# Three pairs of V projections, one block's stores and the last products of a cross-attention layer, rearranged

## The chip, the cores and the metric

The kernel runs on one core of a Trainium2 chip. The metric is device microseconds of one execution of the whole layer. A core has a matrix engine (TensorE, PE in the profile, with its weight loads shown as PEld), a vector engine (VectorE, DVE), a scalar engine (ScalarE, ACT), GpSimd (POOL) and SyncE (SP), which here issues most transfers. Each engine takes its instructions in the order in which the program lists them and waits by semaphores. Products are accumulated in PSUM, which has eight banks of 128 x 512 float32; data lie in SBUF.

## The reference

Four batches, 512 query rows, 512 context rows, width 512, 16 heads of 32, an inner width of 2048, all in float32:

```
x  = layer_norm(hidden) ;  q = x @ q_w + q_b ;  k = enc @ k_w + k_b ;  v = enc @ v_w + v_b
p  = softmax(where(mask, q k^T / sqrt(32), min))       # per head
h  = (p @ v) @ cproj_w + cproj_b + hidden
y  = gelu(layer_norm(h) @ fc_w + fc_b)                 # tanh form
out = h + y @ proj_w + proj_b
```

## The kernel before

Attention is cut into 16 units: a unit `w` is one batch (`w // 4`) and a group of four heads (128 columns). For each unit TensorE makes K (`prep_k`), Q (`prep_q`) and V (`prep_v`), each 128 columns wide. K and Q come out with the head columns on partitions, by four matmuls of 128 x 512. V comes out with the context rows on partitions, by 16 matmuls of 128 x 128 (L285): the context is the stationary side, the 128 columns of `v_w` the moving side. `prep_v_pair` makes V of two units at once, with 16 matmuls of 128 x 256 (L310) into two PSUM banks; each bank is then copied by ACT in two copies, one per unit (L314), and POOL adds the bias to each unit's V (`v_bias`, L321). Before the change units 10 and 11, 12 and 13, 14 and 15 are made so, and units 0 to 9 one by one.

Each unit has two blocks of 256 queries, so there are 32 blocks, `p = 2 * w + half`. In a block, TensorE makes the scores of four heads for two tiles of 128 queries (eight banks, L329); DVE adds the mask and takes each row's minimum of the negated scores (L335); ACT takes the exponential and the row sums (L339); DVE transposes 32 x 32 blocks into a tile `tb` (L347), takes the reciprocal of the sums, ACT spreads it over 32 columns (`rr`, L368), and DVE transposes this too into `tb` (L372). The 32-row blocks then change partitions into `pT` (or into `gt` or `xe`, which serve as further such buffers): POOL copies four of the pieces (L405) and SP issues 12 transfers for the others (L410). Two or three blocks later `attend` multiplies V by them on TensorE (`av`, L429) and DVE divides by the sums into `oT` (L434), which frees the buffer for the next exchange.

While DVE and ACT work on the softmax, TensorE is given other products. A table written by hand, `put(p, items...)`, lists the items of each block with a cost: 3.4 for a projection, 0 for things like a load or a normalisation. `block` calls `fill` at three places: after the last minima of the block (place 0), after the last transposition of `rr` (place 1), and after the exchange has been started (place 2, everything left). At places 0 and 1, `run` takes items while the cost already spent plus half the next one's is at most 3.4, so one projection and the cost-free items right behind it are taken. `next_` gives an item a cost of 0.01, so that it waits for the next place. What ACT and DVE have to do for an item stands in their own order at that place: the bias or copy that empties the bank on ACT, or in block 4 the affine part of batch 1's first normalisation (`ln1_affine`, four activations, L225), which that batch's Q products read.

PSUM banks go round in the order of use. A block uses one bank for `av`, eight for scores, and then one for each product; the first product behind the scores takes the bank of the block's first scores and waits until DVE has taken the minimum from it.

The first MLP layer, and the second for part of the batches, are done by Winograd's form of Strassen's product: seven block products instead of eight, with sums of blocks made ahead. `fc_sums` makes the sums of a pair of `fc_w` tiles on POOL (L622 and L625), ahead of the block that uses them, and for batch 0 stores them to DRAM from POOL's own queue (L714, L715), for the later batches to load. `proj_sums` (`pre`) makes those of a second-layer quarter on POOL; block 14 ends with `pre(0, 0)`.

The last two batches' second layer nests the form twice (`forty_nine`, matmuls of L904). The call named "4" is the last work of the program: seven products, the last two (`s4 w22` and `x22 t4`) into one bank, DVE's additions onto the residual in quarters of 128 x 128, and two stores of 128 x 256 by SP (L1028).

The steps that the change touches are `fc_sums` with the new `late`, `forty_nine`, its last caller in `project`, the `put` lines of blocks 0 to 8, 14 and 29, and the loop that calls `fc_sums`.

Of the kernel before, what the change touches and what calls it, by code (L numbers as in the profile page):

```python
# [53 lines left out]
def xattn_block(ctx: ExitStack, tc: tile.TileContext, x, rawT, encT, mask, q_w, k_w, v_w, c_w, fc_w, p_w, vecs, rows, out):  # L54
# [569 lines left out]
    def add(engine, o, x0, x1):  # L624
        engine.tensor_tensor(o, x0, x1, ALU.add)  # L625
# [77 lines left out]

    def fc_sums(ahead=2):

        while count[3] < len(fc_pairs) and count[3] < count[4] + ahead:
            b, c = fc_pairs[count[3]]
            if ("fcw", b, 2 * c + 1) not in S:
                return
            x, y = raw_pair(b, c)  # L710
            s = wsum[:, count[3] % 2]
            a_sums(x[:, :2], x[:, 2:], y[:, :2], y[:, 2:], s[:, 0], s[:, 1], y[:, :2], s[:, 2], nc.gpsimd)
            if b == 0:
                nc.gpsimd.dma_start(out=sums_dram[c, :, :3], in_=s)  # L714
                nc.gpsimd.dma_start(out=sums_dram[c, :, 3], in_=y[:, :2])  # L715
            S["ws", b, c] = s[:, 0], s[:, 1], y[:, :2], s[:, 2]
            count[3] += 1

    def fc_by_pair(b, c):
# [129 lines left out]
    def last_mlps():  # L849
# [38 lines left out]

        def forty_nine(b, name, o, x, w, free, i, parts=None):

# [24 lines left out]
            if parts:  # L915
                for n, h in enumerate(parts):
                    add(nc.vector, h, o[:, n], h)
            product(r34[:, 0], s4, w22)
            product(r34[:, 1], x22, t4)
            if parts:  # L920
                for n in (1, 2):
                    add(nc.vector, parts[n], r34[:, n - 1], parts[n])
                return
            add(nc.vector, o[:, 1:3], r34[:, :2], o[:, 1:3])
# [13 lines left out]
        def project(b, pairs, sums, turns, middle):  # L938
# [12 lines left out]
            def hid(i, j, t):  # L951
                return S["hid", b, 2 * i + t][:, j * HL : (j + 1) * HL]
# [70 lines left out]
            if b > SPLIT:  # L1023
                parts = [hid(1, 0, t)[:, ts(j, P)] for t in range(2) for j in range(2)]
                middle()
                forty_nine(b, "4", u2p, g22, t4, s3, 5, parts)
                for t in range(2):
                    nc.sync.dma_start(out=out[b, ts(2 + t, P), :HL], in_=hid(1, 0, t))  # L1028
                return
# [73 lines left out]
    def do(fn):  # L1103
        return [(0.0, fn)]

    def next_(fn):
        return [(0.01, fn)]
# [122 lines left out]
    k6, q6, v6 = A(6)  # L1230
    put(0, [(CHAIN, lambda: prep_v(1)), v2], do(lambda: (load_raw(1), store_rn(1))), [k2])
    put(1, [k3, (0.0, lambda: prep_q(1)), (CHAIN, lambda: (prep_v(3), load_enc(1)))], next_(lambda: load_rn(1)))
    put(2, [q2], [q3], do(lambda: ln1_rows(1, 0, 1)))
    put(3, [k4], do(lambda: ln1_rows(1, 2, 3)), [v4])
    put(4, [k5, v5], do(lambda: ln1_affine(1)))
    put(5, [q4, q5])
# [3 lines left out]
    c, t2 = C(0), turns2(0)  # L1240
    put(7, [v6, k], cb(0))
    put(8, x1, [q, v], x4)
    put(9, c[:1], do(lambda: attend(3, 1)), x2[:2], c[1:2], x2[2:], stat(0, 0), c[2:3], stat(0, 1),
# [9 lines left out]
    put(13, [k], some(2))  # L1253
    put(14, [q], some(2), x1, pre(0, 0))
    put(15, some(1), x2[:1], V(10, True), x2[1:2], do(lambda: load_raw(3)), some(2), do(lambda: (store_rn(3), load_rn(3))))
# [21 lines left out]
    put(28, some(3))  # L1277
    put(29, some(1), do(lambda: (fc_sums(), S["late"].pop()())), some(2), do(lambda: (store_out(0), load_mlp())))
    between[14, 1] = lambda: load_mlp(2)
# [5 lines left out]
    for p in range(2 * NW):  # L1285
# [6 lines left out]
        if p > 10:  # L1292
            fc_sums(1 if p == 29 else 2)
        while held_back:
# [73 lines left out]
```

## Time and profile before

| | us |
|---|---|
| median of 3 runs | 757.13 (755.95 to 757.17) |
| profiled execution | 758.21 |
| its span | 756.4 |
| TensorE busy in the span | 748.7 |
| VectorE busy | 617.6 |
| GpSimd busy | 403.6 |
| ScalarE busy | 341.0 |
| V of one unit, behind another projection | 3.57 |
| V of a pair, behind another product | 6.91 |

A row of the profile in order of time has the start and the duration in us, the engine, the line, the operation with output and inputs, shapes, how often it came in a row, and in square brackets the idle time of the engine before it and what ended that. A row of the chain has start, duration and what. A releaser is inferred from semaphore events; where an instruction waits for several, the one that came last is named, and it can be another. SPq and POOLq rows are the issue of a transfer, not its data.

### The profile page before, as it was taken

To read this page: it belongs to the slowest core of one execution; us is meant where nothing else is said; L and a number is where in the kernel's file an instruction comes from. 1 tells how busy PE (TensorE), PEld (TensorE's weight loads), DVE (VectorE), ACT (ScalarE), POOL (GpSimd) and SP (SyncE) were. 2 spreads that over 40 slices of the span, in tenths; PEclk is the share of its full clock that TensorE was granted. 3 is DMA by queue.
4 is the path that set the end of the run, shared out by engine and by line. 5 is a ranking of instruction groups with operands and counts; after the bars stand their busy time and mean duration, and the time that the engine had idled before them with its cause. 6 is when DMAs were issued, how large, how long until landed. Compare 5 with 4: busy or idle time off the path is not lost.

```text
span 756.4 us, 13322 instructions
## 1 busy us (share of the span) xinstructions
PE 748.7 (99%) x4514; PEld 536.2 (71%) x4514; DVE 617.6 (82%) x1229; ACT 341.0 (45%) x776; POOL 403.6 (53%) x401
## 2 busy tenths in 40 slices
PE   9999999999999999999999999999999999999997
PEld 6655555567567546675655776468888899988997
DVE  3889999879988779877987999949877987956865
ACT  2566766555874475648853578401302211022200
POOL 1536837468687987667868974532150014403153
PEclk9999999999999999999999999999999999999999
DMA  8988989467796797676756757766634402046001
GB/s 326 348 238 223 248 208 257 107 191 185 210 255 208 199 268 182 169 193 156 196 129 198 195 145 242 187 213 234 242 104 152 155 13 91 29 162 201 1 15 43
DMA packets 60836, 134.62 MB, mean 178 GB/s; under 512 B 11312, under 2 KB 17072, under 8 KB 60640
## 3 DMA queue, kind: packets, MB, share of 16 engines
q1 hardware_dynamic: 59024, 127.78, 58.7%
q0 software_dynamic: 1600, 5.97, 2.6%
q8 instruction: 36, 0.59, 0.3%
q14 instruction: 32, 0.26, 0.1%
q10 hardware_dynamic: 144, 0.02, 0.0%
HBM read 69.23 MB, written 11.02 MB: 106 GB/s over the span
## 4 chain that ended last, share of the span: by engine, by line
PE 95%; POOL 3%; DMA 1%; issue 0%; SPq 0%; DVE 0%; DVEq 0%; POOLq 0%
PE q L671 24%; PE r L904 10%; PE sc L329 8%; PE av L429 7%; PE acck L262 7%; PE accq L274 7%; PE accc L471 6%; PE accv L285 5%; PE accp L758 4%; PE accv L310 3%; PE q1p L965 2%; PE tp L169 1%; POOL pT L405 1%; PE q3j L777 1%; PE q1j L777 1%; PE q7j L777 1%
## 5 line engine op out<-in xcount | busy, mean ns | idle before, releaser
L339 ACT ACTIVATE ptt<-ptt,mn 128x512 f32<-128x512 f32 x256 | 181.7, 711 | 142.3 <-DVE mn L335 142.3
L335 DVE CUSTOM_DVE_ANT_0 ptt<-sc,mb 128x512 f32<-128x512 f32 x256 | 160.6, 682 | 19.9 <-PE sc L329 19.9
L347 DVE STREAM_TRANSPOSE tb<-ptt 128x1024 f32<-128x1024 f32 x128 | 153.3, 1217 | 0.0
L405 POOL COPY pT<-tb 32x1088 f32<-32x1088 f32 x96 | 104.7, 1091 | 35.1 <-DVE oT L434 11.6
L671 PE MATMUL q<-yT,gt 128*128 128x256 f32 x320 | 78.9, 379 | 0.0
L692 ACT ACTIVATE ga<-ga,vec 128x512 f32<-128x512 f32 x40 | 26.7, 714 | 93.3 <-DVE ga L625 93.3
L671 PEld LDWEIGHTS q<-yT,gt 128*128 128x128 f32 x320 | 60.7, 190 | 8.2
L329 PE MATMUL sc<-pbt 32*128 32x512 f32 x512 | 66.1, 614 | 0.0
L671 PE MATMUL q<-ys,gt 128*128 128x256 f32 x240 | 61.6, 379 | 0.0
L262 PE MATMUL acck<-xe,ptt 128*128 128x512 f32 x128 | 59.1, 605 | 0.0
L274 PE MATMUL accq<-xe,ptt 128*128 128x512 f32 (+1 forms) x136 | 58.1, 573 | 0.0
L671 PEld LDWEIGHTS q<-ys,gt 128*128 128x128 f32 x240 | 45.6, 190 | 6.2
L625 DVE TENSOR_TENSOR ga<-q,ga 128x512 f32<-128x512 f32 (+1 forms) x60 | 36.2, 603 | 15.8 <-PE q L671 12.9
L429 PE MATMUL av<-pT,v 128*32 128x256 f32 x768 | 46.4, 382 | 2.1 <-POOL gt L622 1.9
L339 ACT ACTIVATION_READ_ACCUMULATOR ptt<-ptt,mn 128x1 f32 x256 | 47.8, 187 | 0.0
L274 PEld LDWEIGHTS accq<-xe,ptt 128*128 128x128 f32 x136 | 25.0, 190 | 30.4 <-issue 23.0
L440 POOL TENSOR_TENSOR hid<-hid,row 128x512 f32<-128x512 f32 x18 | 23.5, 1332 | 42.2 <-DMA hid<-xa 42.2
L262 PEld LDWEIGHTS acck<-xe,ptt 128*128 128x128 f32 x128 | 23.4, 192 | 31.6 <-issue 23.0
L329 PEld LDWEIGHTS sc<-pbt 32*128 32x128 f32 x512 | 27.2, 183 | 25.5 <-issue 17.2
L471 PE MATMUL accc<-wc,oT 128*128 128x512 f32 x96 | 42.5, 597 | 0.0
L285 PEld LDWEIGHTS accv<-ptt,xe 128*128 128x128 f32 x320 | 37.0, 192 | 4.9 <-DVE mn L335 2.7
L321 POOL TENSOR_TENSOR v<-v,row 128x512 f32<-128x512 f32 x16 | 20.3, 1280 | 37.1 <-ACT v L290 29.7
(263 smaller groups left out, 1437.2 us busy)
## 6 DMA issues: line engine op xcount, KB each, us to landing
pT<-tb SPq DMA_DIRECT2D x288, 136.0 KB
pbt<-p_w_dram SPq DMA_DIRECT2D x40, 256.0 KB
gt<-ws SPq DMA_DIRECT2D x20, 512.0 KB
gt<-tb SPq DMA_DIRECT2D x48, 136.0 KB
xe<-tb SPq DMA_DIRECT2D x48, 136.0 KB
pbt<-fc_w_dram SPq DMA_DIRECT2D x24, 256.0 KB
gt<-fc_w_dram SPq DMA_DIRECT2D x20, 256.0 KB
ptt<-k_w_dram SPq DMA_DIRECT2D x16, 256.0 KB
```

Source lines behind the costliest of these rows:

```text
L262: nc.tensor.matmul(acc, S["wk", w][:, d, :], eT[:, d, :], start=(d == 0), stop=(d == ND - 1))
L274: nc.tensor.matmul(acc, S["wq", w][:, d, :], xT[:, d, c], start=(d == 0), stop=(d == ND - 1))
L285: nc.tensor.matmul(acc[:, ts(t, P)], eT[:, d, ts(t, P)], S["wv", w][:, d, :], start=(d == 0), stop=(d == ND - 1),)
L329: nc.tensor.matmul(S["sc", w, qt][h], qT[r, ts(qt, P)], kT[r, :], start=True, stop=True)
L335: nc.vector.tensor_tensor_reduce(out=s, in0=S["sc", w, qt][h], in1=S["mb", w // NG], scale=1.0, scalar=FMAX, op0=ALU.add, op1=ALU.min, acc ...
L339: nc.scalar.activation(s, s, AF.Exp, bias=mn, scale=-1.0, accum_out=S["sums", w][:, qt, h : h + 1])
L347: nc.vector.transpose(tv[:, qt % 2, 2 * k : 2 * k + 2], S["ps", w, qt, k])
L405: nc.gpsimd.tensor_copy(pT[ts(i, HD), i], tb[ts(i, HD), i])
L429: nc.tensor.matmul(av[ts(h, HD), : 2 * P].rearrange(shape, **kw), v[:, t, ts(h, HD)], p[t][h], start=(t == 0), stop=(t == NT - 1),)
L471: nc.tensor.matmul(acc, S["oT", b][:, g, ts(t, P)], wc[:, g, :], start=(g == 0), stop=(g == NG - 1))
L671: nc.tensor.matmul(o, x[:, k], y[:, k], start=(k == 0), stop=(k == 1))
L904: nc.tensor.matmul(r, x[:, c], w[:, c], start=(c == 0), stop=(c == NP // 2 - 1))
```

## The change

Three things change.

V of units 2 and 3, 4 and 5, 6 and 7 is made by `prep_v_pair`, in blocks 1, 4 and 8, and the K products of units 2, 3, 5, 7 and the Q product of unit 7 move so that blocks 0 to 8 keep two or three projections' worth of work each. In block 4 the list is now the pair and then the affine part of batch 1's normalisation, without a K product ahead of them; since the pair counts as one item of cost 3.4 and the affine part costs nothing, both are taken at place 0.

The stores of the sums of `fc_w` are put into a list and issued at once, except in block 14, where they are issued after `pre(0, 0)`.

In the last `forty_nine` the two last products get banks of their own, DVE's additions onto the residual are made in halves of two quarters, the store of each part is issued as soon as it is ready, the first two from ACT's queue, the last one, of 128 x 128, from SP's.

```
-    def fc_sums(ahead=2):
+    def fc_sums(ahead=2, hold=False):
...
             if b == 0:
-                nc.gpsimd.dma_start(out=sums_dram[c, :, :3], in_=s)
-                nc.gpsimd.dma_start(out=sums_dram[c, :, 3], in_=y[:, :2])
+                S["late"].append(lambda c=c, s=s, y=y: (
+                    nc.gpsimd.dma_start(out=sums_dram[c, :, :3], in_=s),
+                    nc.gpsimd.dma_start(out=sums_dram[c, :, 3], in_=y[:, :2]),
+                ))
+                if not hold:
+                    late()
...
+    def late():
+        while S["late"]:
+            S["late"].pop(0)()
...
             if parts:
-                for n, h in enumerate(parts):
-                    add(nc.vector, h, o[:, n], h)
+                r4 = half_tile(f"r4{name}_{b}").rearrange("p i (j n) -> p (i j) n", j=2)
+                first, second = parts
+                add(nc.vector, first, o[:, :2], first)
+                product(r34[:, 0], s4, w22)
+                add(nc.vector, first[:, 1], r34[:, 0], first[:, 1])
+                ready(nc.scalar, 0, slice(0, HL))
+                add(nc.vector, second, o[:, 2:], second)
+                ready(nc.scalar, 1, slice(P, HL))
+                product(r4[:, 0], x22, t4)
+                add(nc.vector, second[:, 0], r4[:, 0], second[:, 0])
+                ready(nc.sync, 1, slice(0, P))
+                return
             product(r34[:, 0], s4, w22)
             product(r34[:, 1], x22, t4)
-            if parts:
-                for n in (1, 2):
-                    add(nc.vector, parts[n], r34[:, n - 1], parts[n])
-                return
...
-    put(0, [(CHAIN, lambda: prep_v(1)), v2], do(lambda: (load_raw(1), store_rn(1))), [k2])
-    put(1, [k3, (0.0, lambda: prep_q(1)), (CHAIN, lambda: (prep_v(3), load_enc(1)))], next_(lambda: load_rn(1)))
+    put(0, [(CHAIN, lambda: prep_v(1)), k2], do(lambda: (load_raw(1), store_rn(1))), [k3])
+    put(1, [(CHAIN, lambda: prep_q(1))], V(2), do(lambda: load_enc(1)), next_(lambda: load_rn(1)))
     put(2, [q2], [q3], do(lambda: ln1_rows(1, 0, 1)))
-    put(3, [k4], do(lambda: ln1_rows(1, 2, 3)), [v4])
-    put(4, [k5, v5], do(lambda: ln1_affine(1)))
+    put(3, [k4], do(lambda: ln1_rows(1, 2, 3)), [k5])
+    put(4, V(4), do(lambda: ln1_affine(1)))
...
-    put(7, [v6, k], cb(0))
-    put(8, x1, [q, v], x4)
+    put(7, [k, q], cb(0))
+    put(8, x1, V(6), x4)
...
-    put(14, [q], some(2), x1, pre(0, 0))
+    put(14, [q], some(2), x1, pre(0, 0), do(late))
...
-    put(29, some(1), do(lambda: (fc_sums(), S["late"].pop()())), some(2), do(lambda: (store_out(0), load_mlp())))
+    put(29, some(1), do(lambda: (fc_sums(), late())), some(2), do(lambda: (store_out(0), load_mlp())))
...
-            fc_sums(1 if p == 29 else 2)
+            fc_sums(1 if p == 29 else 2, p == 14)
```

More of the change, by code (lines that the diff above doesn't have):

```diff
@@ L887, in x_sums, with forty_nine @@
             sub(s4, x12, s2, nc.gpsimd)
-        def forty_nine(b, name, o, x, w, free, i, parts=None):
+        def forty_nine(b, name, o, x, w, free, i, parts=None, ready=None):
             x11, s3, x12, x22 = quarters(x)
@@ L1023, in project @@
             if b > SPLIT:
-                parts = [hid(1, 0, t)[:, ts(j, P)] for t in range(2) for j in range(2)]
+                parts = [hid(1, 0, t).rearrange("p (j n) -> p j n", j=2) for t in range(2)]
                 middle()
-                forty_nine(b, "4", u2p, g22, t4, s3, 5, parts)
-                for t in range(2):
-                    nc.sync.dma_start(out=out[b, ts(2 + t, P), :HL], in_=hid(1, 0, t))
+                forty_nine(
+                    b, "4", u2p, g22, t4, s3, 5, parts,
+                    lambda q, t, c: q.dma_start(out=out[b, ts(2 + t, P), c], in_=hid(1, 0, t)[:, c]),
+                )
                 return
```

## The prediction

> **What bounds the kernel now.** I read the page's busy times first, then the chain that ended last, then, around each edited place, the rows of the engines in order of time.
>
> ```profile
> PE 748.7 (99%) x4514; PEld 536.2 (71%) x4514; DVE 617.6 (82%) x1229; ACT 341.0 (45%) x776; POOL 403.6 (53%) x401
> PE 95%; POOL 3%; DMA 1%; issue 0%; SPq 0%; DVE 0%; DVEq 0%; POOLq 0%
> ```
>
> TensorE is busy for 748.7 of 756.4 us and carries 95% of the chain; the granted clock is 1.00 in every stretch asked. So an edit is worth the TensorE time that it removes, plus or minus the waits that it takes from TensorE or gives to it. The profiled execution took 758.21 us, 1.8 more than its span and 1.08 more than the median of the three runs (757.13). I make the sum against 758.21 and move the median by the same amount. A measurement of this kernel hardly tells less than 0.2%, 1.5 us, from no change.
>
> **V of units 2 to 7 by pairs.** What V costs is in the chain (start, duration, what):
>
> ```profile
> 103.56 3.77 PE accv L285 x32
> 118.22 3.57 PE accv L285 x32
> 324.67 7.11 PE accv L310 x32
> 376.56 6.91 PE accv L310 x32
> ```
>
> One unit alone takes 3.57 us, a pair 6.91. The first item after the scores pays 0.20 more in both forms (3.77, 7.11); some item stands there in any layout, so that cancels. Six units alone are 21.42 us, three pairs 20.73: TensorE loses 0.69 us of work. Twice the width costs almost twice the time, so pairing buys 3%.
>
> The Trainium skill, page "TensorE: Matmul & The Clock Gate", section "Back-to-back issue gap", gives 81 ns for a weight load with a matmul 128 columns wide, and 109 ns by its formula for 256 columns alone. Their ratio, 109/162, would bring 21.42 us down to 14.4, a gain of 7.0 us against 0.69 by the rows. The trace has the pair itself, at 6.91, so it doesn't agree.
>
> The weights of the pairs are asked for early enough: unit 3's load follows unit 1's V, which still stands first in block 0, and the pair runs in block 1 behind a query product; the other loads follow the pair three or more blocks before their use. POOL gets the two bias additions of a pair together (1.28 us each) in front of a pT or gt copy; the attention that needs the copy is two blocks away, so I cost that at nothing, and at one block's wait of 1.3 us if that distance were gone. Moving K products between blocks moves items of 3.43 to 3.63 us, and each edited block's TensorE work falls by 0.09 to 0.15 us.
>
> **ACT's order in block 4.** This is the part that speaks against the change. The rule that fills blocks takes the pair at the price of one item, at the first of its three places, and then the free item behind it too: the four affine activations of batch 1 (L225). At that place ACT comes to them before the copy rr (L368). In the old order they stood at the second place, behind rr. Block 4 before, ACT, then DVE, then TensorE:
>
> ```profile
> 77.44 0.71 ACT L339 ACTIVATE ptt<-ptt,mn 128x512 f32<-128x512 f32 x1
> ...
> 78.14 0.67 ACT L264 ACTIVATE pbt<-acck,vec 128x512 f32<-128x512 f32 x1
> 78.71 0.39 ACT L368 COPY rr<-rsum 128x256 f32<-128x256 f32 x1
> 79.00 0.58 ACT L290 COPY v<-accv 128x512 f32<-128x512 f32 x1
> 79.48 2.93 ACT L225 ACTIVATE xe<-raw,vec 128x512 f32<-128x512 f32 x4
> 82.31 0.71 ACT L339 ACTIVATE ptt<-ptt,mn 128x512 f32<-128x512 f32 x1
> ```
>
> ```profile
> 79.56 0.40 DVE L372 STREAM_TRANSPOSE tb<-rr 128x256 f32<-128x256 f32 x1
> 79.94 0.42 DVE L434 TENSOR_TENSOR oT<-av,pT 128x256 f32<-128x256 f32 x1
> 80.97 0.69 DVE L335 CUSTOM_DVE_ANT_0 ptt<-sc,mb 128x512 f32<-128x512 f32 x1 [0.60 <-PE sc L329]
> ```
>
> ```profile
> 79.81 2.00 PE L329 MATMUL sc<-pbt 32*128 32x512 f32 x16
> 81.81 1.53 PE L274 MATMUL accq<-xe,ptt 128*128 128x512 f32 x3
> ```
>
> Two more prices, the four copies of a pair, and how soon DVE follows rr where ACT is the late one (block 1):
>
> ```profile
> 331.93 1.16 ACT L314 COPY v<-accv 128x256 f32<-128x256 f32 x4
> 44.78 0.40 ACT L368 COPY rr<-rsum 128x256 f32<-128x256 f32 x1
> 45.21 0.45 DVE L372 STREAM_TRANSPOSE tb<-rr 128x256 f32<-128x256 f32 x1
> ```
>
> ACT is through its exponentials at 78.14. The pair's matmuls end 7.11 us after the scores of their block, at about 77.9, so the copies don't wait for them. Four copies take about 1.10 us back to back (79.24), the affine ones 2.83 (79.48 to 82.31), so rr starts at 82.07 in place of 78.71. DVE's transposition of rr follows 0.43 later, at 82.50, 2.94 us later than now. Behind it on DVE, in this order, stand the division into oT (0.38 later) and the first minimum of the next block (0.42 after that): 83.30 in place of 80.97. DVE's idle 0.60 has absorbed that much. TensorE's next item, the query product of unit 4, needs the bank which that minimum frees; it followed the minimum by 0.84 (80.97 to 81.81), so it starts at 84.1. TensorE waits 2.3 us, and block 4's own 0.09 saving drowns in the wait: V is worth 0.60. TensorE is late for good, since nothing downstream waited in this stretch. Bounds: nothing if the row order on ACT turned out otherwise; 2.94 if DVE's 0.60 slack were used elsewhere. I take 2.3, nearest to the rows. Block 8 has the same form with a plain load behind the pair instead of ACT work: rr comes 0.5 us later there, the transposition about 0.1, which the 0.6 of DVE idle covers.
>
> **Block 14's stores.** TensorE's largest wait, 1.86 us, stands ahead of the attention of pair 13. TensorE, then SP's transfers into pT one block earlier and in this block, then POOL, then a store's landing:
>
> ```profile
> 203.64 1.93 PE L429 MATMUL av<-pT,v 128*32 128x256 f32 x32
> ...
> 216.16 1.03 PE L671 MATMUL q<-ys,pbt 128*128 128x256 f32 x4
> 219.04 1.93 PE L429 MATMUL av<-pT,v 128*32 128x256 f32 x32 [1.86 <-POOL gt L622]
> ```
>
> ```profile
> 192.69 7.50 SPq L410 DMA_DIRECT2D pT<-tb  x12
> ...
> 206.15 8.47 SPq L410 DMA_DIRECT2D pT<-tb  x12
> ```
>
> ```profile
> 214.08 0.56 POOL L714 DMA_DIRECT2D ws<-wsum  x1 [0.30 <-POOL wsum L622]
> 214.65 0.54 POOL L715 DMA_DIRECT2D ws<-pbt  x1
> 215.20 1.29 POOL L625 TENSOR_TENSOR ptt<-gt 128x512 f32<-128x512 f32 x1
> 216.44 1.28 POOL L622 TENSOR_TENSOR ptt<-pbt 128x512 f32<-128x512 f32 x1
> 217.66 1.28 POOL L622 TENSOR_TENSOR gt<-gt 128x512 f32<-128x512 f32 x1
> ```
>
> ```profile
> ws<-wsum POOLq DMA_DIRECT2D x1, 384.0 KB, 4.8
> ```
>
> The attention reads pT and v, not gt, so the named releaser, which ends at 218.94, may only be the event that fell nearest. In block 13 the attention started 10.95 us after the first pT transfer was issued, without a wait; the same distance here gives 217.10, before TensorE was ready (216.16 + 1.03). Here the issue took 0.97 longer, and the stores of POOL, 512 KB with 4.8 us to landing, began at 214.08, while pT was still under way. The change sets the two stores behind the four subtractions and additions of POOL: they start near 219.1, with pT landed. If the stores made the last pT transfer late, all 1.86 goes; if POOL's operation itself were the releaser, it comes 1.10 earlier (0.56 + 0.54) and as much goes; if pT was late by its own slow issue, nothing goes. I take 1.86, with 0 kept as the other end. The stores then delay POOL's next pT copies by 0.5 us or less, and share the engines with x loads; the attention that needs that pT comes after block 15, 21 us long.
>
> The Trainium skill, page "DMA: Bandwidth & Descriptors", section "SWDGE vs HWDGE vs iDMA", says that software and hardware descriptors feed different queues inside each DMA engine, between which it alternates. By that rule a store begun before pT has landed takes turns with it, the gain of 1.86; without it the stores would queue behind, and the gain would be 0. The longer issue and the wait agree with it, but block 13's stores, started as late after the issue, did no harm.
>
> **The last products.** The end of the program, TensorE, DVE, SP:
>
> ```profile
> 751.09 1.06 PE L904 MATMUL r<-row,ga 128*128 128x128 f32 x8
> ```
>
> ```profile
> 746.46 1.43 DVE L625 TENSOR_TENSOR hid<-p1p,hid 128x256 f32<-128x256 f32 x4
> ...
> 750.40 0.75 DVE L625 TENSOR_TENSOR u2p<-r,u2p 128x256 f32<-128x256 f32 x2 [1.29 <-PE r L904]
> 751.07 0.88 DVE L625 TENSOR_TENSOR hid<-u2p,hid 128x128 f32<-128x128 f32 x4
> 752.19 0.49 DVE L625 TENSOR_TENSOR hid<-r,hid 128x128 f32<-128x128 f32 x2 [0.23 <-PE r L904]
> ```
>
> ```profile
> 752.54 0.81 SPq L1028 DMA_DIRECT2D out_dram<-hid  x2
> ```
>
> TensorE's work is the same. After its last product two small additions (0.49) and two issues (0.81) follow one another; after the change one addition (0.25) and one issue of SP (0.41), the others having gone out on ACT's queue about 0.4 us earlier. DVE's additions before that are two of 0.36 and one of 0.25 from 751.1, done by 752.1, in time for the last product at 752.15. The last issue starts near 752.5 instead of 752.95: 0.45 us. No row has an ACT store at the end, so the bounds are 0 (ACT's stores land last) and 0.81 (the whole issue).
>
> **The sum.** -0.60 (V) + 2.3 (rr behind the affine ones) - 1.86 (pT) - 0.45 (end) = -0.61 us. The profiled 758.21 would be 757.6, the median 757.13 becomes 756.5, less than 0.1% down.
>
> **The rivals.**
> The wait in block 14 stays (slower). Mechanism: pT's last transfer is late by its own issue, 8.47 us against 7.50, and the stores had little part in it. Place: the attention of pair 13. Price: the 1.86 is not gained, -0.60 + 2.3 - 0.45 = +1.25, 758.4 us. For it: the longer issue, and block 13's harmless stores; against it: 8.47 - 7.50 explains only 0.97 of the 1.86. It decides the sign as soon as less than 1.25 of the wait goes, and passes 0.2% where the end brings under 0.2.
> DVE's lateness in block 4 is hidden (faster). TensorE would go on with the query product at 81.8; -0.69 - 1.86 - 0.45 = -3.0, 754.1 us. For it: ACT is busy 45% only; against it: the three rows of DVE, which take their work in order, and the bank that only DVE frees.
> Weight loads bound the narrow V and the pairs go at a third less: 14.4 for 21.42 us, another 6.3 off the sum, 750 us. Against it: pairs at 6.91.
> A wait elsewhere, from the reshuffled loads and biases of blocks 0 to 8, of the size of one late POOL copy (1.09 to 4.5 us): with 2 us, 758.5 us and more.
>
> **How the numbers follow.** The sum as written, its wait in block 14 mostly gone: 0.47. The wait stays: 0.28, half of it past +1.5 us. The lateness hidden: 0.15. Weight loads: 0.01. A wait elsewhere: 0.09. Faster by over 0.2%: 0.15 + 0.01 and 0.06 of the first case (the end's 0.81 and a smaller wait in block 5), 0.22. Slower by over 0.2%: 0.15 + 0.09, 0.24. Within: 0.54. The likeliest case alone spans 755.4 to 757.7. The range reaches from the hidden case (754.1) to the wait that stays with no gain at the end and 2.94 in block 5 (757.13 - 0.60 + 2.94 = 759.5), which leaves the extreme ends out: 753.9 to 759.2.
>
> **What would show it.** Three groups of L310 more, each 6.9 to 7.1 us. In block 4 ACT's rr starts some 3.4 us later against the block's scores, DVE idles before L372 on ACT, and TensorE has a wait of about 2.3 us ahead of the query product of block 5. The 1.86 ahead of pair 13's attention is gone, with POOL's stores after its four operations. The last store is issued about 0.4 us after the last product. Wrong would be: no idle time of DVE before L372 in block 4; the wait before pair 13's attention still there; a new wait in another block.

## The result and the profile after

| | before | after |
|---|---|---|
| median of 6 runs, us | 757.15 (755.95 to 758.48) | 761.79 (760.73 to 764.49) |
| ratio, 95% interval | | 1.0066 (1.0049 to 1.0084) |
| profiled execution, us | 758.21 | 763.2 |
| its span, us | 756.4 | 761.4 |

The change makes the kernel 4.6 us slower. 756.5 had been forecast, with a range from 753.9 to 759.2. The two spans differ by 5.0 us. First the page after: the engines' busy times, the chain that ended last, and the group of the paired V products (busy us and mean ns of one).

```profile
PE 753.0 (99%) x4418; PEld 534.2 (70%) x4418; DVE 618.2 (81%) x1225; ACT 341.7 (45%) x782; POOL 402.8 (53%) x401
PE 94%; DMA 2%; DVE 1%; SPq 1%; ACT 1%; POOL 1%; issue 0%; DVEq 0%; POOLq 0%
L310 PE MATMUL accv<-ptt,xe 128*128 128x256 f32 x192 | 42.7, 381 | 0.0
```

TensorE has 96 matmuls fewer and 4.3 us more of busy time. Busy time that grows while the work shrinks points to a clock. Its rows in block 5 and behind, in order of time, then who kept it waiting (total us, times, longest):

```profile
78.81 2.90 PE L329 MATMUL sc<-pbt 32*128 32x512 f32 x14
84.48 2.07 PE L329 MATMUL sc<-pbt 32*128 32x512 f32 x2 [2.77 <-DVE oT L434]
86.48 9.12 PE L274 MATMUL accq<-xe,ptt 128*128 128x512 f32 x16
95.53 1.93 PE L429 MATMUL av<-gt,v 128*32 128x256 f32 x32
```

```profile
PE sc L329 <- DVE oT L434: 2.8, 1, 2.8
```

From the first score product of block 5 to the attention behind it TensorE takes 16.72 us (78.81 to 95.53). Before it took 9.03 (79.81 to 88.84). That is 7.69 us lost in one block, and it is made of two things. The first is DVE's lateness:

```profile
74.94 2.37 DVE L347 STREAM_TRANSPOSE tb<-ptt 128x1024 f32<-128x1024 f32 x2 [2.12 <-POOL pT L405]
83.67 0.45 DVE L372 STREAM_TRANSPOSE tb<-rr 128x256 f32<-128x256 f32 x1 [2.81 <-ACT rr L368]
84.35 0.67 DVE L335 CUSTOM_DVE_ANT_0 ptt<-sc,mb 128x512 f32<-128x512 f32 x1
```

```profile
79.37 1.17 ACT L314 COPY v<-accv 128x256 f32<-128x256 f32 x4
80.41 2.93 ACT L225 ACTIVATE xe<-raw,vec 128x512 f32<-128x512 f32 x4
83.24 0.40 ACT L368 COPY rr<-rsum 128x256 f32<-128x256 f32 x1
```

DVE takes block 5's first minimum at 84.35, 5.54 us after the first score product; before it did so 1.16 after it (80.97 against 79.81). The difference, 4.38, is the forecast wait for `rr` (2.81, forecast 2.94), plus one that was not in the sum, 2.12 for POOL's copy of `pT`, less the 0.6 of slack (4.33; the last 0.05 is spread over the rows).

TensorE meets this lateness one step earlier than forecast, not ahead of the query product but ahead of the last two score products. They fill the bank that `av` held, which DVE's division into `oT` frees, just in front of that minimum. Where the clock holds, the query product starts 1.05 us behind these two (vw_affine_ahead, below). Here that would have been at 84.48 + 1.05 = 85.53, 6.72 us after the first score product in place of 2.00. So the lateness costs TensorE 4.7 us.

The second thing is the clock. Windows of 3 us over the same place (stretch, length, busy of PE, PEld, DVE, ACT and POOL, then the granted clock):

```profile
81.00:84.00 3.00, 0.71 (x3) 0.00 (x0) 0.33 (x1) 2.64 (x5) 2.88 (x4) 0.95 0.88 256
84.00:87.00 3.00, 2.52 (x3) 0.99 (x4) 3.00 (x11) 1.93 (x5) 2.92 (x3) 0.50 0.47 111
87.00:90.00 3.00, 3.00 (x4) 1.01 (x3) 3.00 (x6) 2.41 (x8) 2.92 (x4) 0.50 0.98 229
90.00:93.00 3.00, 3.00 (x8) 1.43 (x7) 3.00 (x8) 2.00 (x6) 1.59 (x2) 0.92 0.85 199
```

TensorE's clock is halved shortly before 84 and full again at about 90.5: 0.3 + 6.0 + 0.5 = 6.8 us at half speed. TensorE works through 6.0 of them, from 84.48 on, and loses half of that. The query product takes 9.12 us where the same 16 matmuls took 7.1. Of the 7.69 us, 4.7 are lateness and 3.0 the clock.

Not every execution lost that much. The profiled one has a mean granted clock of 0.996, and so has one other (763.20 and 764.49 us). The other four have 0.998 and a median of 761.4. A mean of 0.998 leaves room for at most 3.8 us at half speed (0.0025 x 761 x 2), which costs 1.9.

The Trainium skill, page "TensorE: Matmul & The Clock Gate", section "What's actually happening", describes a gate that halves the clock after an idle window of about 3.4 us and opens it after a busy one, on windows that run free. The trace agrees with the halving, and the length of the fall, 6.8 us, is that of two such windows; in pairs_only, below, it is 3.4, one window. The products had been away for only 2.77 us, less than the page's window, but the score products before it were sparse too.

Where does the late copy of `pT` come from? SP's issues, what the issues of the exchange waited for (between 44 and 64 us), then POOL, of the kernel after:

```profile
46.49 0.84 SPq L251 DMA_DIRECT2D ptt<-v_w_dram  x2
49.63 10.60 SPq L410 DMA_DIRECT2D gt<-tb  x12
60.28 1.07 SPq L216 DMA_DIRECT2D hid<-rn  x2
```

```profile
SPq L410 <- DMA xe<-encT_dram: 3.5, 4, 1.4
```

```profile
64.76 1.28 POOL L221 TENSOR_TENSOR raw<-raw,hid 128x512 f32<-128x512 f32 x1 [11.03 <-DMA hid<-rn]
70.44 4.47 POOL L405 COPY pT<-tb 32x1088 f32<-32x1088 f32 x4
```

and of the kernel before, with DVE's transposition at the end:

```profile
47.06 0.33 SPq L251 DMA_DIRECT2D ptt<-v_w_dram  x1
49.39 8.92 SPq L410 DMA_DIRECT2D gt<-tb  x12
58.35 1.07 SPq L216 DMA_DIRECT2D hid<-rn  x2
```

```profile
SPq L410 <- DMA xe<-encT_dram: 1.9, 4, 0.9
```

```profile
68.70 4.47 POOL L405 COPY pT<-tb 32x1088 f32<-32x1088 f32 x4
73.72 2.37 DVE L347 STREAM_TRANSPOSE tb<-ptt 128x1024 f32<-128x1024 f32 x2
```

POOL does the first normalisation's raw rows (L221) ahead of that copy. They wait for the statistics' rows (`hid<-rn`, L216), which SP issues behind the exchange of block 1. That exchange waits for the context rows (`encT`) to land, 3.5 us in all where it was 1.9. These stand behind the loads of weights. After the change two loads of `v_w` come right ahead of them where there was one, but with the loads of `k_w` and `q_w` it is four loads of 256 KB in both kernels; they are issued within 1.97 us (45.36 to 47.33) in place of 2.97 (44.42 to 47.39). That the closer loads make the context rows late is an argument; what taking loads away does is measured below. Before, POOL was through at 73.17, 0.55 us ahead of DVE's need; after, SP issues L216 1.93 later and POOL is 2.12 late.

The other two parts did what was forecast in this profile. The wait in block 14 is gone: the attentions of pairs 12 and 13 are 13.47 us apart, before 15.40 (203.64 to 219.04).

```profile
210.10 1.93 PE L429 MATMUL av<-pT,v 128*32 128x256 f32 x32
223.57 1.93 PE L429 MATMUL av<-pT,v 128*32 128x256 f32 x32
```

And the span ends 3.63 us after the last product (756.71 + 1.06 = 757.77) in place of 4.25:

```profile
756.71 1.06 PE L912 MATMUL r<-row,ga 128*128 128x128 f32 x8
757.57 0.82 ACTq L1042 DMA_DIRECT2D out_dram<-hid  x2
758.28 0.33 SPq L1042 DMA_DIRECT2D out_dram<-hid  x1
```

### The profile page after: what moved, and what is told of

It reads as the page before. It is cut to its first block, busy times and chain, and to the rows that moved or that the text cites. A ratio compares the mean times of both kernels' runs of the same rounds, so it can differ in the third digit from the quotient of the medians.

```text
span 761.4 us, 13142 instructions
## 1 busy us (share of the span) xinstructions
PE 753.0 (99%) x4418; PEld 534.2 (70%) x4418; DVE 618.2 (81%) x1225; ACT 341.7 (45%) x782; POOL 402.8 (53%) x401
## 4 chain that ended last, share of the span: by engine, by line
PE 94%; DMA 2%; DVE 1%; SPq 1%; ACT 1%; POOL 1%; issue 0%; DVEq 0%; POOLq 0%
PE q L671 25%; PE r L912 10%; PE sc L329 8%; PE av L429 7%; PE accq L274 7%; PE acck L262 6%; PE accc L471 6%; PE accv L310 5%; PE accp L766 4%; PE q1p L979 2%; PE accv L285 2%; PE tp L169 1%; PE q3j L785 1%; PE q1j L785 1%; PE q5j L785 1%; PE q7j L785 1%
## 5 line engine op out<-in xcount | busy, mean ns | idle before, releaser
L347 DVE STREAM_TRANSPOSE tb<-ptt 128x1024 f32<-128x1024 f32 x128 | 153.3, 1217 | 2.3 <-POOL pT L405 2.1
L329 PE MATMUL sc<-pbt 32*128 32x512 f32 x512 | 69.9, 617 | 2.8 <-DVE oT L434 2.8
L274 PE MATMUL accq<-xe,ptt 128*128 128x512 f32 (+1 forms) x136 | 60.1, 589 | 0.0
L310 PE MATMUL accv<-ptt,xe 128*128 128x256 f32 x192 | 42.7, 381 | 0.0
```

Of the source, the lines that this page charges most:

```text
L274: nc.tensor.matmul(acc, S["wq", w][:, d, :], xT[:, d, c], start=(d == 0), stop=(d == ND - 1))
L310: nc.tensor.matmul(acc[:, t], eT[:, d, ts(2 * i + t, P)], wv[:, d], start=(d == 0), stop=(d == ND - 1))
L329: nc.tensor.matmul(S["sc", w, qt][h], qT[r, ts(qt, P)], kT[r, :], start=True, stop=True)
L347: nc.vector.transpose(tv[:, qt % 2, 2 * k : 2 * k + 2], S["ps", w, qt, k])
```

## The experiments

Each kernel's time stands against runs of the kernel before on the same chip. The lengths of blocks are differences between the starts of successive blocks' first score products in the profiles; before, block 4 takes 11.00, block 5 10.90, block 14 15.39. The last column counts the executions whose mean granted clock was 0.998 or lower. A fall of 3.4 us to half speed gives 1 - 1.7/757 = 0.9977, one of 6.8 us 0.9955. The clock also falls behind the last product, where it costs nothing (in the profile of stores_only from 752.1 on, mean 0.9986), so the count is not exact: 3 of the 111 executions of the kernel before that stand beside these kernels are at 0.998.

| kernel | median, us | before, us | ratio (95%) | block 4 | block 5 | block 14 | clock low |
|---|---|---|---|---|---|---|---|
| the change | 761.79 | 757.15 | 1.0066 (1.0049 to 1.0084) | 10.90 | 18.58 | 13.47 | 6 of 6 |
| pairs_only | 762.34 | 756.83 | 1.0070 (1.0051 to 1.0089) | 10.90 | 16.27 | 13.47 | 5 of 6 |
| stores_only | 756.46 | 756.83 | 0.9994 (0.9985 to 1.0002) | 11.00 | 10.96 | 13.47 | 0 of 11 |
| end_only | 756.72 | 756.83 | 0.9993 (0.9977 to 1.0008) | 10.99 | 10.90 | 13.47 | 0 of 12 |
| stores_end | 756.22 | 756.82 | 0.9989 (0.9976 to 1.0001) | 11.00 | 11.63 | 13.47 | 0 of 12 |
| affine_behind | 757.24 | 756.83 | 1.0010 (0.9999 to 1.0022) | 10.90 | 11.86 | 13.47 | 2 of 12 |
| affine_ahead | 758.99 | 756.66 | 1.0024 (1.0008 to 1.0040) | 10.99 | 13.02 | 13.46 | 4 of 12 |
| affine_split | 760.18 | 756.66 | 1.0039 (1.0019 to 1.0059) | 11.31 | 16.14 | 13.47 | 7 of 12 |
| affine_twice | 766.20 | 756.82 | 1.0125 (1.0102 to 1.0148) | 10.99 | 18.27 | 13.47 | 5 of 5 |
| rows_first | 760.84 | 756.66 | 1.0041 (1.0026 to 1.0056) | 12.86 | 13.02 | 13.47 | 5 of 12 |
| rows_first_behind | 758.31 | 756.66 | 1.0013 (1.0002 to 1.0024) | 13.08 | 10.90 | 13.46 | 0 of 11 |
| rn_scalar | 758.57 | 756.82 | 1.0019 (1.0007 to 1.0031) | 12.92 | 10.90 | 13.47 | 3 of 12 |
| vw_behind | 755.62 | 756.82 | 0.9982 (0.9968 to 0.9997) | 10.90 | 10.90 | 13.47 | 1 of 12 |
| vw_affine_ahead | 760.33 | 756.56 | 1.0047 (1.0029 to 1.0066) | 10.90 | 13.45 | 13.47 | 5 of 8 |
| vw_single | 755.39 | 756.56 | 0.9974 (0.9962 to 0.9986) | 10.99 | 11.03 | 13.46 | 0 of 12 |

### Which part carries the loss

pairs_only is the kernel before with the new lists of blocks 0, 1, 3, 4, 7 and 8:

```
-    put(4, [k5, v5], do(lambda: ln1_affine(1)))
+    put(4, V(4), do(lambda: ln1_affine(1)))
...
```

> The kernel before with the pairs and the new lists of blocks 0 to 8 alone (affine activations ahead of rr); stores and end as before. Both theories: it carries the whole loss, 757.15 + 7.6 - 0.5 = about 764 us. If it were below 760, the loss would be in the stores or the end instead.

In its profile TensorE waits 2.60 ahead of the last two score products of block 5, and the clock falls for half as long as in the changed kernel's profile: the share missing from 1.00, times 3 us and doubled, gives 1.6 + 1.9 = 3.4 us at half speed.

```profile
84.00:87.00 3.00, 2.73 (x4) 1.03 (x5) 3.00 (x10) 2.13 (x7) 2.92 (x4) 0.74 0.53 120
87.00:90.00 3.00, 3.00 (x6) 1.27 (x5) 3.00 (x6) 2.21 (x7) 2.92 (x4) 0.69 0.80 188
```

stores_only is the kernel before with `hold` and `late`:

```
+                S["late"].append(lambda c=c, s=s, y=y: (
...
-    put(14, [q], some(2), x1, pre(0, 0))
+    put(14, [q], some(2), x1, pre(0, 0), do(late))
```

> The kernel before with block 14's stores held back alone. The prediction's reading, the stores make the last pT transfer late: the wait before pair 13's attention goes, 757.15 - 1.9 = 755.3 us. Rival, pT is late by its own issue: the wait stays, 757.1.

end_only has only the new end of the last `forty_nine`:

```
+                ready(nc.scalar, 0, slice(0, HL))
...
+                ready(nc.sync, 1, slice(0, P))
```

> The kernel before with the new end alone. Prediction: one issue and one small addition less behind the last product, 0.45 us; the profile of the changed kernel shows 3.6 us from the last product to the end of the span against 4.2, so 0.6: about 756.6 us. Rival, the stores from ACT land last and nothing is gained: 757.15.

The lists of the pairs carry the whole loss, 5.5 us. The stores and the end together (stores_end, the change with the old lists) gain 0.6 us, at the edge of what these runs can tell:

> The kernel before with the two parts of the change that are not the pairs: block 14's stores held back, and the last products and stores in the new order. If the two are worth what the times of each alone gave (0.4 and 0.1 to 0.4), the sum is 0.5 to 0.8 under the kernel before: 756.0 to 756.4; if neither is worth anything, no difference.

In a typical execution the stores' 1.86 us were not there to be won. In stores_only pair 13's attention follows as soon as in the changed kernel:

```profile
203.42 1.93 PE L429 MATMUL av<-pT,v 128*32 128x256 f32 x32
216.89 1.93 PE L429 MATMUL av<-pT,v 128*32 128x256 f32 x32
```

But so it does in pairs_only and end_only, whose stores stand where they stood before, with the same 13.47. Of the 16 profiles only that of the kernel before has the wait, and that execution was 1.08 us over its median. In this respect the profile was not a picture of the typical run. What made the wait there stays open in part. SP's issue of the transfers took 8.47 us in it, with the stores in their old place. In stores_only the issue took as long, 8.59, and there is no wait, so a slow issue alone doesn't make one. In the four other profiles with the stores in their old place it took 7.50 to 7.98.

### ScalarE's order

affine_behind is the changed kernel with the affine activations one place later, behind `rr`:

```
-    put(4, V(4), do(lambda: ln1_affine(1)))
+    put(4, V(4), next_(lambda: ln1_affine(1)))
```

> The changed kernel with one edit: in block 4 the four affine activations get the small price that makes them wait for the next place, so that ACT comes to them behind rr. Theory 1, ACT's order in block 4 is the cause: DVE no longer idles before L372, TensorE has no wait in block 5 and no clock drop behind it, the 7.6 us lost between the scores of block 4 and the attention behind block 5 come back, and the kernel is near 757.15 - 0.6 - 1.9 - 0.6 = 754 us. Theory 2, the pairs and their loads are the cause (POOL's late pT copy holds DVE up before L347): TensorE still waits about 2 us in block 5, the clock still drops, and the time stays above 757.

This takes back most of the loss: 0.66% becomes 0.10%, 4.2 us less. TensorE's wait of 2.77 and the half clock are gone. Without the 2.3, the prediction's other terms would give 754.2, and the kernel is still 0.4 above before, within the interval. DVE's wait for POOL is still there, 1.13 in its profile, and block 5 takes 11.86:

```profile
73.99 2.37 DVE L347 STREAM_TRANSPOSE tb<-ptt 128x1024 f32<-128x1024 f32 x2 [1.13 <-POOL pT L405]
```

affine_ahead asks for the opposite: the kernel before, unit by unit, with that order alone.

```
-    put(4, [k5, v5], do(lambda: ln1_affine(1)))
+    put(4, [k5], do(lambda: ln1_affine(1)), [v5])
```

> The kernel before, with the four affine activations of block 1 (L225) moved ahead of V of block 5 in the list of block 4, so that ScalarE runs them ahead of the copy of the row sums as in the changed kernel; nothing else of the change is in it. If ScalarE's order alone carries the loss, the copy of the row sums comes about 2.9 us later, VectorE's lateness less the 0.6 it can absorb makes TensorE wait about 2.3 us in block 5, and the time is 757.0 + 2.3 = 759.3; if that wait is also enough to halve the granted clock as in the changed kernel, another 3.2, so 762. If the late copy of GpSimd (pT) is needed as well, which in the kernel before was on time by 0.55 us, the time is 757 to 758 and the clock stays at 1.0.

The price of the order is 2.33 us by the medians, as the prediction's step had it (2.3). The eight executions whose clock held have a median of 758.73, which is 2.1 above before, and block 5 is 2.12 longer. DVE, then TensorE:

```profile
82.33 0.45 DVE L372 STREAM_TRANSPOSE tb<-rr 128x256 f32<-128x256 f32 x1 [2.31 <-ACT rr L368]
```

```profile
80.09 1.99 PE L329 MATMUL sc<-pbt 32*128 32x512 f32 x12
82.83 1.43 PE L329 MATMUL sc<-pbt 32*128 32x512 f32 x4 [0.74 <-ACT v L290]
84.18 7.13 PE L274 MATMUL accq<-xe,ptt 128*128 128x512 f32 x16
```

The edit also puts V of unit 5, with ACT's copy of it (L290), behind the activations. That copy, which the row names, ends at 82.77; the division into `oT`, which the last two score products need, ends at 83.07. So DVE's lateness alone is enough for the delay. The clock holds here (the query product takes 7.13). It was low in 4 of 12 executions, two of which are the slowest, 762.2 and 762.8; the other two took 759.2 and 759.8.

affine_split halves the dose in the changed kernel:

```
-    put(4, V(4), do(lambda: ln1_affine(1)))
+    put(4, V(4), do(lambda: ln1_affine(1, (0, 1))), next_(lambda: ln1_affine(1, (2, 3))))
...
```

> The changed kernel with two of the four affine activations of block 1 ahead of the copy of the row sums and two behind it: half of ScalarE's delay, 1.5 us in place of 2.9. If the loss were in proportion to the delay, it would lie half way between 757.2 (all four behind) and 761.8 (all four ahead): 759.5. If the granted clock decides, it either still halves (761.8 - 1.5 = 760.3) or it does not: then the lateness of 4.4 - 1.5 = 2.9 leaves at most 2.9 - 1.4 of wait over the version with all four behind, and the time is 757.2 to 758.7 with a clock of 1.0 in blocks 4 and 5.

Its median lies between the cases, but its executions are of two kinds: five with a mean granted clock of 0.999 or 1.0 took 756.8 to 758.4, median 757.5, and seven at 0.995 to 0.998 took 759.7 to 763.4, median 761.1. Same program, same chip: 3.6 us apart. The clock explains at most a part. The profiled execution, 763.44, is of the second kind, and its fall lasts 3.4 us (granted clock 0.93 from 84 to 87 and 0.51 from 87 to 90), which costs 1.7. It also has more lateness than the others with these lists, 2.73 ahead of the transposition where affine_behind has 1.13:

```profile
76.72 2.37 DVE L347 STREAM_TRANSPOSE tb<-ptt 128x1024 f32<-128x1024 f32 x2 [2.73 <-DMA ptt<-k_w_dram]
```

Whether the executions of the first kind had less of this wait, no profile shows. affine_twice prices the fall without pairs or late rows:

```
-    put(4, [k5], do(lambda: ln1_affine(1)), [v5])
+    put(4, [k5], do(lambda: (ln1_affine(1), ln1_affine(1))), [v5])
```

> The version of the kernel before that has only the affine activations ahead of the row sums (758.99 against 756.66), with these four activations executed twice (the second execution writes the same values), so that ScalarE's delay is 5.9 us in place of 2.9; no pairs, loads as before. It prices the granted clock by itself. If TensorE's wait costs its length alone, the time is 759.0 + 2.9 = 761.9 with a granted clock of 1.0. If a wait of 3 us and more halves the clock for some 6.8 us afterwards, as in blocks 4 and 5 of the changed kernel, 3.4 more: 765.3, and a mean granted clock of .995 to .996 in every execution.

766.2: the version that counts the clock was 0.9 off, the one that counts the wait alone 4.3. The mean granted clock is 0.994 to 0.996 in all five. The rows of its TensorE, and windows there (the clock is 0.95 from 81 to 84, so the fall lasts 0.3 + 6.0 + 0.5 = 6.8 us again):

```profile
84.98 2.38 PE L329 MATMUL sc<-pbt 32*128 32x512 f32 x4 [3.45 <-ACT v L290]
87.29 8.73 PE L274 MATMUL accq<-xe,ptt 128*128 128x512 f32 x16
```

```profile
84.00:87.00 3.00, 2.02 (x4) 0.81 (x4) 2.52 (x9) 2.05 (x6) 2.28 (x3) 0.50 0.21 46
87.00:90.00 3.00, 3.00 (x5) 1.18 (x4) 3.00 (x10) 3.00 (x9) 2.88 (x4) 0.50 0.93 215
90.00:93.00 3.00, 3.00 (x8) 1.43 (x7) 3.00 (x7) 1.41 (x5) 0.74 (x1) 0.91 0.93 212
```

### The late rows

DVE's wait ahead of block 4's transposition (L347) varies between executions. With the pairs' lists it is 2.12 in the changed kernel, 1.03 in pairs_only, 1.13 in affine_behind and 2.73 in affine_split. Unit by unit, with the loads where they were, there is none in four profiles (before, end_only, affine_ahead, affine_twice), 0.45 in stores_only and 1.12 in stores_end. So the profiles with the pairs' lists have more of it, and 2.12 is not the size of every run.

If the load of the statistics' rows is late because it stands behind the exchange, putting it ahead should help. rows_first does this in the changed kernel, rows_first_behind in affine_behind:

```
-    put(1, [(CHAIN, lambda: prep_q(1))], V(2), do(lambda: load_enc(1)), next_(lambda: load_rn(1)))
+    put(1, [(CHAIN, lambda: prep_q(1))], V(2), do(lambda: load_rn(1)), do(lambda: load_enc(1)))
```

> The changed kernel with the load of the normalised rows of block 1 issued ahead of the load of the encoder rows and of the exchange that SyncE issues, so that VectorE's raw row (L221) and GpSimd's copy of pT (L405) are not held up; the affine activations stay ahead of the row sums. If the late copy of GpSimd carries 2.1 us of the lateness of 4.4 us, that part goes: 759.7 if the clock still halves in block 5, 756.5 if the shorter wait leaves it at 1.0. If the order on ScalarE carries all, the time stays at 761 to 762 although GpSimd's copy starts at 69 instead of 70.4.

> Both remedies: the load of the normalised rows ahead, and the affine activations behind the row sums. If the two are the whole loss, what is left is the gain of the parts: V by pairs (-0.6), the stores (-0.4) and the end (-0.1 to -0.6), so 755.5 to 756.0 against 757.0 before, and no wait over 0.5 us on VectorE in blocks 4 and 5. If the load is not the cause of the rest, it stays at the 757.2 of the version with the affine activations behind alone.

It didn't: rows_first keeps most of the loss, and rows_first_behind, at 758.31, is above both its numbers. Block 5 lost its late copy, and block 4 got a wait of the same size (12.86 and 13.08 in place of 10.90). DVE of rows_first_behind:

```profile
65.30 2.37 DVE L347 STREAM_TRANSPOSE tb<-ptt 128x1024 f32<-128x1024 f32 x2 [2.39 <-DMA gt<-tb]
```

Half a megabyte in front of the exchange (`gt<-tb`) makes the exchange late, and DVE waits for the `tb` that it frees. In rows_first the wait is 2.16; its row names POOL's copy, but that had ended 0.68 earlier.

rn_scalar leaves the exchange's place on SP alone and lets ACT's queue issue that load, in affine_behind:

```
...
-    put(1, [(CHAIN, lambda: prep_q(1))], V(2), do(lambda: load_enc(1)), next_(lambda: load_rn(1)))
-    put(2, [q2], [q3], do(lambda: ln1_rows(1, 0, 1)))
+    put(1, [(CHAIN, lambda: prep_q(1))], V(2), do(lambda: load_enc(1)))
+    put(2, do(lambda: load_rn(1, nc.scalar)), [q2], [q3], do(lambda: ln1_rows(1, 0, 1)))
```

> The changed kernel with the affine activations behind the row sums, and the load of the normalised rows of block 1 issued by ScalarE's queue in block 2 (about 53 us), in place of by SyncE behind the exchange of pair 1 (about 59.4 us). If the rest of the loss is that load's place behind the exchange, VectorE's raw rows' operands land some 4 us earlier, GpSimd's copy of pT starts at 68 or before, VectorE does not wait for it, and the time is 755.5 to 756.2, below the kernel before in the same call. If it is the loads' number or something later, 757.2 as with the affine activations behind alone.

A miss as well: block 4 takes 12.92. SP's issues of the exchange now wait 2.5 us for that very load:

```profile
SPq L410 <- DMA hid<-rn: 2.5, 1, 2.5
```

So the rows' own place is not what is wrong. The other possibility is that the stretch has too much ahead of the exchange. vw_behind, again in affine_behind, takes bytes away from there: the two loads of `v_w`, which nothing needs before block 4, go behind the rows.

```
-    put(1, [(CHAIN, lambda: prep_q(1))], V(2), do(lambda: load_enc(1)), next_(lambda: load_rn(1)))
+    put(1, [(CHAIN, lambda: prep_q(1))], [(CHAIN, lambda: prep_v_pair(2, load=False))], do(lambda: load_enc(1)),
+        next_(lambda: (load_rn(1), load_w(4, names=("wv",)), load_w(5, names=("wv",)))))
...
```

> The changed kernel with the affine activations behind the row sums, and the two loads of v_w that the pair of units 2 and 3 issues moved behind the load of the normalised rows. If the rest of the loss (757.2 against 755.5 to 756.0 by the sum of the parts) comes from the exchange of pair 1, whose issues on SyncE wait for the 1 MB of encoder rows, then 0.5 MB less ahead of them (1.3 us at 390 GB/s) lets them end a microsecond earlier, GpSimd's copy of pT starts at 68.5 or before, VectorE's wait of 1.1 for it is gone, and the time is 756.2. If the rest has another cause, it stays at 757.2.

755.62, 0.6 under the 756.2 expected, and below the kernel before. The rows are issued 3.5 us earlier than in the changed kernel, POOL copies `pT` at 65.85 in place of 70.44, and DVE doesn't wait (this kernel's lines from 317 on are numbered one higher):

```profile
56.75 1.08 SPq L216 DMA_DIRECT2D hid<-rn  x2
60.69 5.22 POOL L221 TENSOR_TENSOR raw<-raw,hid 128x512 f32<-128x512 f32 x4 [6.71 <-DMA hid<-rn]
65.85 4.47 POOL L406 COPY pT<-tb 32x1088 f32<-32x1088 f32 x4
73.15 2.37 DVE L348 STREAM_TRANSPOSE tb<-ptt 128x1024 f32<-128x1024 f32 x2
```

Two questions were left. Is the order enough for the fallen clock when the rows are in time? vw_affine_ahead is vw_behind with the activations ahead again (`do` for `next_` in block 4).

> The changed kernel with the two loads of v_w moved behind the normalised rows, and the affine activations left ahead of the row sums: ScalarE's order without the late rows. If the order costs TensorE 2.3 us by itself, as in the kernel before with the order alone, the time is 755.6 + 2.3 = 757.9, with a granted clock of 1.0 in most executions. If the order alone is enough in the paired layout for the longer wait and the halved clock, 755.6 + 5.5 = 761.1.

Neither number: 760.33. In its profile the wait is 1.48 and the clock holds (1.00 from 84 to 97); block 5 is 2.55 longer.

```profile
83.40 1.12 PE L330 MATMUL sc<-pbt 32*128 32x512 f32 x2 [1.48 <-DVE oT L435]
84.45 7.13 PE L274 MATMUL accq<-xe,ptt 128*128 128x512 f32 x16
```

In 5 of 8 executions the clock is low, and those have a median of 760.99. So the order alone brings the paired layout to the edge; with the late rows, in the changed kernel and pairs_only, the clock is low in 11 of 12.

And whose is the gain of vw_behind? vw_single is stores_end, unit by unit, with the one load of `v_w` of V of unit 3 moved behind the rows:

```
-    put(1, [k3, (0.0, lambda: prep_q(1)), (CHAIN, lambda: (prep_v(3), load_enc(1)))], next_(lambda: load_rn(1)))
+    put(1, [k3, (0.0, lambda: prep_q(1)), (CHAIN, lambda: (prep_v(3, False), load_enc(1)))],
+        next_(lambda: (load_rn(1), load_w(5, names=("wv",)))))
...
```

> The version without pairs that has the stores and the end of the change (756.22), with the one load of v_w that V of unit 3 issues moved behind the normalised rows. If the late rows cost the old layout too (its profile shows VectorE waiting 1.12 for GpSimd's copy of pT in one execution), the time falls by up to 1: 755.3 to 756.2, and then the pairs alone are worth the difference to 755.6, 0 to 0.6. If the late rows are a matter of the pairs' layout, it stays at 756.2.

755.39: the lowest median of all, and it has no pairs. Against stores_end the moved load gains 0.15% by the ratios, but their intervals overlap. In the two profiles the rows are issued 0.55 earlier (58.49 against 59.04) and block 5 is 0.60 shorter, although the exchange waits no less for the context rows (3.2 against 2.4). The 0 to 0.6 us expected for the pairs came out on the other side, 0.2 us (0.9982 against 0.9974), inside the intervals. The pairs do save what the rows promised: in the profiles blocks 0 to 4, 7 and 8 of vw_behind and vw_single differ by -0.14, -0.10, 0.00, -0.14, -0.09, -0.13 and -0.10, in sum 0.70 us (block 5, 0.13 longer in vw_single, has a wait there). Blocks 16 and 18 take it back. Over all profiles block 16 has a mean of 17.54 with pairs (nine profiles) and 16.98 without (seven), block 18 14.39 and 13.72. The two together take 31.44 to 32.92 with pairs and 30.47 to 31.09 without, so every profile with pairs is longer there, by 1.2 us in the mean. Why that is, no run here shows; it stays open.

## Why the prediction was wrong

- **V by pairs, -0.60.** The size held: 381 ns a matmul, 0.70 us over blocks 0 to 8 in the profiles, and not the 7.0 that the Trainium skill's cadence would have made (page "TensorE: Matmul & The Clock Gate", section "Back-to-back issue gap"). In the times of whole runs it isn't seen: blocks 16 and 18, which the prediction didn't look at, take 1.2 more with pairs.
- **ACT's order, +2.3: the step that failed.** The lateness was right: DVE waits 2.81 for `rr` (2.94 forecast), 0.6 is absorbed, and alone the order costs 2.1 to 2.3 us (affine_ahead). TensorE's wait stands one step earlier than forecast, at the bank of `av`. Two things were missing. "The granted clock is 1.00 in every stretch asked" was taken from a profile that had no TensorE wait of this kind; a wait made by the change has its own clock, and it cost 3.0 us in the profiled execution and up to 1.9 in the four at 0.998. And the 2.3 was added up as if `rr` were the only lateness in the block: the loads were put at nothing.
- **The loads, rival "a wait elsewhere", 0.09.** It named the mechanism, one late POOL copy, and its size (2 us), as an alternative to the sum, priced at 2 us and more. It came on top of the late `rr`, on the same DVE queue in the same block. Together they made lateness of 4.38 in the profile, and the clock was low in all six executions. The prediction's "the weights of the pairs are asked for early enough" looked at when the loads' own readers need them, and not at what waits behind them on SP.
- **Block 14's stores, -1.86.** This term was mis-sized. Of the 16 profiles only that of before has the wait. By the times the stores are worth 0.4, within the interval (0.9994, 0.9985 to 1.0002). The rival that it stays was asked as a question about the change, when it was one about the profile. Whether the two kinds of DMA queue alternate, which stood behind it, no run here shows.
- **The end, -0.45.** 0.62 in the profile; by the times 0.9993 (0.9977 to 1.0008), so between 0 and 1.

By ratios, in us of 757: the order with its clock +4.2 (0.56%, the change to affine_behind); the late rows +2.1 (0.28%, affine_behind to vw_behind), of which the layout unit by unit pays 1.1 as well (0.15%, stores_end to vw_single), so +1.0; stores and end -0.8 (0.11%); pairs +0.6 (0.08%, vw_single to vw_behind), which agrees with 0.7 saved and 1.2 given back. The sum is the 5.0 of the ratio 1.0066; it must be, since each step starts where another ends. Only the first term is clear of the noise. For the 2.1 the two intervals just stand apart (0.9999 to 1.0022, 0.9968 to 0.9997), for the 1.1, and so for the +1.0, they overlap, and the last two terms are within the intervals of their comparisons.

## What to carry over

A wait that a change puts on TensorE can cost more than its length: behind waits of 1.4 to 3.5 us in sparse work four profiles here show the clock at half for 3.4 or 6.8 us, 1.7 to about 3 us more, so lateness has to be added up over all waits on the same engine's queue before it is called affordable. A load moved for its own reader's sake must also be costed for what waits behind it in the queue and on the engines: here moving 256 or 512 KB from ahead of an exchange was worth 1.1 or 2.1 us by the ratios, and the rearranged products 0.7. And a wait in one profile is worth its size only if the runs that lie at the median have it too.

## What the hardware showed that was not expected

The clock falls in pieces of one length. In the four profiles that have a fall before the last product it lasts 3.4 us (pairs_only, affine_split) or 6.8 (the change, affine_twice). Whether it falls is partly a matter of chance. The mean clock is low in 3 of 111 executions of the kernel before, in 4 and 5 of 12 of affine_ahead and rows_first, in 5 of 8 of vw_affine_ahead, in 7 of 12 of affine_split, and in 16 of 17 of the change, pairs_only and affine_twice. Nor does the length of the wait alone decide: TensorE waited 1.37 us ahead of the fall in affine_split's profile and 1.48 in vw_affine_ahead's, where the clock held. And the fall can begin when the wait is over: in pairs_only TensorE is at work again from 84.27, and the clock falls at about 85.4 (1.56 us ahead of 87). Windows of about 3.4 us that run free, as the Trainium skill's page "TensorE: Matmul & The Clock Gate", section "What's actually happening", has them, would give the lengths, the chances and the late start; the runs show these, not the windows. Nor was it expected that a load moved to another engine's queue (rn_scalar) stays in the way of SP's exchange, which then waited 2.5 us for it.
